# Spread rows of a four-layer graph attention kernel: through DRAM and ScalarE instead of TensorE transposes

## The chip, the cores and the metric

The kernel runs on one core of a Trainium2 chip. A core has five engines, each with its own in-order queue of instructions: TensorE (PE, matrix products and transposes; its weight loads are listed as PEld), VectorE (DVE), ScalarE (ACT), GpSimd (POOL) and SyncE (SP), which here issues every transfer. They work on SBUF (128 partitions) and on PSUM, where TensorE leaves its results; the DMA engines move data between SBUF and DRAM. The metric is the device time of one execution in microseconds, lower is better.

## What is computed

x is (32, 512, 256), float32: 32 graphs (batches) of 512 nodes with 256 features; adj is one 512x512 matrix of 0 and 1 for all of them. Four layers of graph attention follow each other, each on a normalised input and with a residual:

```python
h = jnp.maximum(_layernorm(x, axis=-1), 0.0)
x = x + layer(h, adj, ...)

# layer 0: four heads of 64 features, slope 0.2
e = s_src[:, :, None, :] + s_dst[:, None, :, :]
e = jnp.where(e > 0, e, 0.2 * e)
e = jnp.where(mask, e, -jnp.inf)
alpha = jax.nn.softmax(e, axis=2)
out = elu(einsum('bijh,bjhd->bihd', alpha, Wh))

# layer 1: a dense layer to 512, attention over all nodes (no mask) on 512 features,
# elu, residual, a dense layer to 256, attention with the mask, elu, residual, relu
# layer 2: one head of 256, slope 0.2, mask with the diagonal, elu
# layer 3: one head of 256, slope 0.01, mask, relu
```

Each attention weight is exp(leaky(s_i + t_j) + mask_ij - peak_i), divided by its sum over j. s and t are one number per node, two columns of a product with the layer's weights.

## The kernel before

**Tiles.** A batch stands in SBUF as 128 partitions x 4 tiles of nodes x 256 features (`xt`). Its numbers per node (s, t and what follows from them) are columns: 128 partitions x 4. To add s_i and t_j for a whole 128x512 tile of weights, one of the two must lie along the free dimension in all 128 partitions: a *spread row*, 128x512, each partition with the same 512 numbers.

**Two ways to a spread row.** `spread` (L632) makes it with TensorE: four transposes (L409) of a column, broadcast to 128x128, into a PSUM tile `row`. `lines` (L638) with `row_of` (L652) makes it through DRAM: one transpose (L643) turns the columns into a few partitions, ScalarE copies them to SBUF (`turned`), SP writes them to DRAM as `line` (L647), and SP reads the line back, broadcast to 128 partitions, into an SBUF tile `rb` of 256 KB (L655).

**Where they are used, per batch.**
- `peaks` (L658): spread of t, then for each of four node tiles one VectorE instruction (L665) that adds the mask and takes the maximum. Called for each of four heads, and once in each of three `gat`.
- `weights_T` (L694): `row_of` for cb (slope x s - top), spread for ca (s - top). For each of four tiles VectorE (L708) makes max(ca + (1 - slope) t, cb), GpSimd (L718 or L726) adds the mask, ScalarE (L719 or L733) takes the exponential into `pt`, which is the next product's weights. Called once a head and once a `gat`.
- `full_gat_T` (L838, no mask): the maximum of t over all nodes by a reduction (L859), one broadcast transpose and another reduction (L862); then `low_row` through DRAM and `t_row` by transposes (L886, L887) from the exponentials `c`; after the sums, `r_row` through DRAM and `q_row` by transposes (L908, L909).

The columns themselves come from `score_columns` (L678). Products are issued by `product` (L413); a product of 32-bit numbers is two matmul instructions in the profile, a transpose is one.

**The order.** Nothing is issued as the functions call it. `do` records each operation with its engine and an estimated duration, and `Plan.order` (L211) plays the recording: five batches are admitted at a time (`DEPTH`), each engine takes the ready operation with the lowest key, and tiles come from pools with a fixed number of slots (`SLOTS`: 7 of PSUM, 14 of the kind that holds `rb` and `y`). Keys are `max(0, b - 1) * PERIOD - urgency - add` with one urgency per operation of a batch (`URGENCY`, `FIRST` for the first graph recorded, and `EARLY` and `LAST` for the first and last three batches). The result is one fixed order for each engine. A matmul that is followed in this play by a gap of PE of at least 400 ns gets fillers, transposes of the identity into a PSUM tile that nothing reads (L1040):

```python
before.fill = int(FILL * gap / FILL_NS) if gap >= FILL_FROM else 0   # 0.6, 110, 400
```

A transfer is played with `max(n / 290, 300)` ns on SP, and lands 2500 ns later (900 for one of up to 8 KB).

Of the kernel before, what the change touches and what calls it, by code (L numbers as in the profile page):

```python
# [17 lines left out]
P = 128  # L18
# [18 lines left out]
PERIOD = 102900  # L37
# [7 lines left out]
    124187, 27458, 54024, 85815, 127927, 143082, 328815, 201328, 391462, 117691, 172181, 188793, 424644,  # L45
    248357, 290339, 151093, 548898, 347549, 249382, 346103, 190819, 493927, 189995, 235067, 375057, 312531,
    137476, 244237, 15588, 99471, 384419, 49912, 229134, 263406, -53868, 164326, 315017, 150418, 189541,
    87635, 113355, 113764, 92446, 180536, 315464, 22239, 104163, 37445, 153709, 69377, -33292, 57871, 68049,
    126632, 69380, 719561, 411345, -24739, 362683, 348747, 125710, 203386, -121226, 187184, 138735, 353972,
    479768, 379305, 100152, 225429, 177495, 202483, 437896, 179455, 177379, 459436, 207363, 251462, 276418,  # L50
    273051, 72134, 190340, 87240, 87462, 139994, 240070, 193165, 284099, 65171, 190882, -134531, 105489,
    204215, 436695, 354960, 84403, 365091, 388125, 158735, 132975, 125189, 140317, 28490, 135519, -133251,
    154984, 88833, 200704, 326910, 157401, -73420, 186088, 84030, 65473, 259435, 167820, 250548, 296226,
    155732, 148751, 184404, 102606, 47275, -89101, 109929, -22866, 120917, 132180, 72833, 179715, 293811,
    220306, 251604, 160377, -54812, 503963, 294348, 299648, 310480, 184310, 214427, 108134, 113382, 77944,
    -25259, 220915, 140253, 225101, 210070, 131593, -58641, 24901, 144922, 103834, -55042, -75773, 164955,
    51925, 37449, -37331, 194373, 165595, -53550, 134891, 73360, 200944, 169423, 370536, 148147, -8567,
    38227, 46537, -53506, 90629, 156363, 38013, 136307, 242309, 268100, 181379, 540681, 343781, 13085,
    106358, 381623, 252693, 34895, 86342, 41729, 145874, 57439, 180188, 371373, 144376, 113078, 212804,
    -56127, 175395, 39766, 20079, 122711, 16968, 81730, 36363, 33992, -9360, 244377, -16060, 173755, 812,  # L60
    195516, 96125, 24952, -99232, -256301, -273097, -325559, -217701, 62283, 41197, -317611, 121173,
    -573678, 24884, 161520, 281482, 42489, 132062, -71349, 206084, 127481, 161080, 218323, 174535, 382862,
    102363, 138949, -461371, 156706, 104313, 110685, 23741, 36809, 245583, 241597, 127455, 108694, 188549,
    189532, 121772, -38178, 162471, 73800, -52269, -68603, 102738, -10655, -40955, 2651, -65771, -94520,
    -132306, -380612, -101522, 98486, -36866, 305416, 62454, 65218, 94847, 204499, -47196, -74891, 216006,
    116703, -2381, -35719, -54275, -88533, -61935, 162867, -43915, 33052, -66202, 300499, -32636, 366366,
    327210, 59123, -165649, -89201, -347471, -174109, 44450, -340320, -322205, 336730, 425930, -331413,
    -60472, 15548, -236854, 64799, -286767, 264655, 136916, -210240, -130968, -69939, 4579, -163881,
    -114273, 229104, -3917, 51351, -164012, 71327, 184751, 34354, 88349, 218844, 73114, -114468, -63532,
    -85563, 244008, -87751, 209096, 276106, 219920, -137361, -89605, -131850, 241785, 82900, -208551,  # L70
    408441, 219935, -120937, -86266, -303126, 83675, 342059, 247005, 270933, 343321, 445672, 32970, 226125,
    -99438, 421870, 210292, 244826, 111374, 326504, 91555, -198928, -201687, -117310, 106781, -204532,
    67380, 99851, 66174, 191938, 283427, -85698, 6999, -8041, -95104, 177690, 102217, 25471, -7218, -47609,
    83544, -176267, 249182, -156218, -42446, -271332, 96408, -67700, 346080, -176537, -62170, -305860,
    -184573, -145498, -147352, 117568, -69973, 118138, -249506, 368017, 13506, -339817, -119489, 20691,
    -348133, -79577, -84578, 6007, 307149, -307611, -145956, -183471, -15732, 140957, -255635, -382374,
    11304, -58674, 49007, 69987, -197223, -465279, -170466, -47363, -177944, -100942, -227476, -459555,
    -35943, -374495, -161886, -188736, -213550, -478756, -113477, -237771, 114174, 25915, -203660, -235706,
    -62347, -49597, -119568, -276148, -278214, -571867, -240723, -472941, -276555, -150856, -178488,
    -125457, 51835, -119700, -113894, -198170, -267546, 913, 117494, 256204, 145580, 376286, 209102, 171461,  # L80
    165583, 1669, 258510, 19824, 278900, -103101, 178925, -9332, -105670, 172239, -297204, -161311, 107839,
    -80060, -168358, -503089, 286564, 116767, -326016, 36349, -42523, -373280, 52721, -549613, -185149,
    -350665, -263248, -524205, -114044, -425175, -394279, -290405, -98380, -283605, -656628, -503163,
    -332603, -466007, -238943, -479060, -312439, -461877, -761392, -824734, -834926, -757956, -1420966,
    -867896, -996520, -1174568, -1123798, -565242, -880525, -1056087, -1150294, -548818, -562165, -896349,
]
FIRST = [
    150625, 66367, -80914, 492852, 578582, 373790, 355233, 415411, 370342, 690632, 394774, 315517, 353203,
    129880, 197161, 432376, 789236, 500119, 645039, 728290, 726809, 782644, 812030, 1227229, 554726, 440195,
    427374, 520046, 670466, 709727, 194712, 543582, 496069, 321884, 91730, -45145, -92106, -199160, -149565,  # L90
    -369576, -525217, 119569, -25360, -315873, -515466, -503797, -111924, -325457, -83298, -69769, -254726,
    -424755, -154683, -114778, -101144, -419674, -490772, -341279, -218775, -354199, -315242, -499839,
    -403835, -279297, -179333, -63778, -215266, -305608, -132642, -176645, -343457, -55095, -344188, -79362,
    -182571, -64104, -353103, 2550, -407651, -228043, -371846, -353326, -107818, -171068, -352557, 71238,
    -155665, -77756, 69351, 83846, -64981, -152757, -173901, -107973, -117670, -664153, -331667,
# [3 lines left out]
    [350911, 4027, 95729, 276014, 659, -22230, 139089, 81698],  # L99
    [64803, 14957, 3729, -92060, -58664, 505679, 18595, -112320],  # L100
    [19486, -119307, -73079, 207604, 52200, 207194, -142315, -3205],
]
LAST = [
    [221588, 144111, 158140, 151755, 738851, -328217, 140264, 837366],
    [95908, 48069, 135713, 252237, -167477, -708999, 206689, 139833],
    [-4997, 24600, 39765, 70813, -84122, 447504, -165822, -554656],
# [226 lines left out]
def gat_stack(  # L333
# [298 lines left out]
    def spread(cols, holds=()):  # L632

        row = Later("ps", "row", [P, N])
        transposes(row.all, [cols(t).view(lambda a: a.to_broadcast([P, P])) for t in range(NT)], holds)
        return row

# [14 lines left out]
    def row_of(line, n):  # L652

        row = Later("b2", "rb", [P, N])
        transfer(row.all, [line[n : n + 1]], 4 * P * N, lambda o, a: nc.sync.dma_start(out=o, in_=a.to_broadcast([P, N])))  # L655
        return row

    def peaks(t_col, far, peak):  # L658

        row = spread(t_col)  # L660
        for it in range(NT):
            left = Later("b1", "left", [P, N], BF16)

            def run(o, junk, a, far):
                return nc.vector.tensor_tensor_reduce(  # L665
                    out=junk,
                    in0=a,
                    in1=far,
                    scale=1.0,
                    scalar=LOWEST,  # L670
                    op0=ALU.add,
                    op1=ALU.max,
                    accum_out=o,
                )

            do(DVE, 690, [peak(it), left.all], [row.all, far[:, it, :]], run)

    def score_columns(s, t, peak, lift, slope, shape):  # L678
# [3 lines left out]
        u, top, ca, cb, cc, ct = (Later("tiny", n, [P, *shape]) for n in ("u", "top", "ca", "cb", "cc", "ct"))  # L682
# [5 lines left out]
        do(DVE, 78, [ca.all], [s, top.all], lambda o, a, b: nc.vector.tensor_tensor(o, a, b, ALU.subtract))  # L688
        do(DVE, 78, [cb.all], [s, top.all], lambda o, a, b: stt(o, a, slope, b, ALU.mult, ALU.subtract))
        do(POOL, 200, [cc.all], [t], lambda o, a: nc.gpsimd.tensor_scalar(o, a, 1.0 - slope, None, ALU.mult))  # L690
        do(POOL, 200, [ct.all], [t], lambda o, a: nc.gpsimd.tensor_scalar(o, a, slope, None, ALU.mult))
        return ca, cb, cc, ct

    def weights_T(ca, line_b, cc, ct, farT, even):  # L694

# [395 lines left out]
```

## Time and profile before

Three runs took 3389.28, 3391.61 and 3391.96 us. One more execution was profiled.

| what | value |
|---|---|
| median of the runs | 3391.61 us |
| the profiled execution, its own time | 3391.39 us |
| its span, first to last instruction | 3389.6 us |
| mean granted TensorE clock | 0.999 |
| PE busy in the first 100 us | 81.22 us |
| PE busy in the last 40 us (3350 to 3390) | 32.13 us |
| PE busy from 500 to 3000 us | 2491.92 of 2500 us |
| `rb` rows read back, 256 KB each | 288 |
| `line` writes, 2 KB / 8 KB | 160 / 32 |
| row transposes of L409 | 2080 |
| line transposes of L643 | 192 |
| share of 16 DMA engines in the middle | 0.11, 34 GB/s |

How to read the lines below: a group line gives the source line, the engine, the operation, what is written from what, the shapes and the count, then busy microseconds, the mean duration of one in ns, and the idle time of the engine just before these instructions with what ended it. A timeline line gives start, duration, engine and group. A waits line gives the waiting instruction, what ended the wait, and the total, the number and the longest of such waits in microseconds. A matmul's duration holds the time in which the next ones already run behind it.

### The profile page before, as it was taken

How to read it: one execution, taken by the hardware profiler on the slowest of the kernel's cores; microseconds unless marked ns; L12 is line 12 of the kernel's file. 1: busy time of each engine (PE TensorE's matmuls, PEld its weight loads, DVE VectorE, ACT ScalarE, POOL GpSimd, SP SyncE). 2: the span in 40 equal slices, each digit the busy share in tenths (PEclk: the TensorE clock that was granted, in tenths of full speed). 3: DMA queues.
4: the chain of work that ended last, by engine and by line, in shares of the span. 5: the costliest groups of instructions: out<-in, count | busy, mean ns of one | idle time of the engine just before them, and what ended most of it. 6: DMA issues, size and time to landing. Idle time of an engine off the chain costs nothing. (4 is left out here: it accounts for less than half of the span.)

```text
span 3389.6 us, 52024 instructions
## 1 busy us (share of the span) xinstructions
PE 3348.1 (99%) x17313; PEld 2610.8 (77%) x17313; DVE 2732.0 (81%) x8008; ACT 2122.0 (63%) x4269; POOL 1483.5 (44%) x1801
## 2 busy tenths in 40 slices
PE   7999999999999999999999999999999999999998
PEld 7867777777777777877778777777877788777777
DVE  8777788888878888878888878888887888789576
ACT  4556666666666666665676565666665666666565
POOL 4433444344444445443445443444443454454244
PEclk9999999999999999999999999999999999999999
DMA  3000011101110101101011101011101011110011
GB/s 125 32 10 29 27 40 29 38 23 38 41 38 29 35 26 38 41 32 33 25 36 42 38 29 38 23 38 42 38 29 35 23 41 39 35 40 23 13 32 35
DMA packets 82828, 118.76 MB, mean 35 GB/s; under 512 B 7808, under 2 KB 44288, under 8 KB 82560
## 3 DMA queue, kind: packets, MB, share of 16 engines
q1 hardware_dynamic: 82560, 115.44, 10.9%
q8 instruction: 137, 2.24, 0.3%
q14 instruction: 131, 1.07, 0.1%
HBM read 98.04 MB, written 17.37 MB: 34 GB/s over the span
## 5 line engine op out<-in xcount | busy, mean ns | idle before, releaser
L726 POOL TENSOR_TENSOR y<-y,farT_some 128x512 f32<-128x512 f32 x512 | 591.4, 1180 | 375.7 <-DVE y L708 372.9
L419 PE MATMUL mm<-v,pt 128*128 128x257 f32 x3072 | 698.8, 381 | 1.4 <-ACT pt L719 0.5
L708 DVE SCALAR_TENSOR_TENSOR y<-row,cc,rb 128x512 f32<-128x512 f32 x896 | 619.5, 741 | 48.8 <-DMA rb<-line 40.7
L419 PEld LDWEIGHTS mm<-v,pt 128*128 128x128 f32 x3072 | 571.4, 190 | 89.5 <-ACT pt L719 4.2
L733 ACT ACTIVATE pt<-y,ct 128x512 f32<-128x512 f32 x640 | 455.9, 716 | 149.1 <-POOL y L726 141.7
L419 PEld LDWEIGHTS mmh<-vh,pt 128*128 128x128 f32 x4096 | 482.7, 192 | 10.2 <-ACT pt L733 3.7
L419 PE MATMUL mmh<-vh,pt 128*128 128x65 f32 x4096 | 484.7, 272 | 1.9 <-ACT pt L733 1.8
L419 PE MATMUL mm<-wfc,out1T 128*128 128x256 f32 (+1 forms) x2048 | 468.6, 380 | 0.0
L419 PE MATMUL mm<-ptf,hfc 128*128 128x512 f32 x1024 | 456.8, 594 | 0.0
L665 DVE CUSTOM_DVE_ANT_0 left<-row,far_nz 128x512 bf16<-128x512 f32 x640 | 416.3, 683 | 25.0 <-PE row L409 24.4
L718 POOL TENSOR_TENSOR y<-y,g 128x512 f32<-128x512 f32 x256 | 328.9, 1302 | 243.8 <-ACT g L714 214.3
L419 PEld LDWEIGHTS mm<-wfc,out1T 128*128 128x128 f32 x2048 | 380.6, 189 | 51.7 <-issue 0.5
L624 ACT ACTIVATE h<-xt,shift,rstd 128x256 f32<-128x256 f32 x512 | 275.6, 592 | 173.6 <-DVE shift L616 166.3
L419 PEld LDWEIGHTS mm<-ptf,hfc 128*128 128x128 f32 x1024 | 187.9, 190 | 199.9 <-issue 192.1
L726 POOL TENSOR_TENSOR y<-y,farT_self 128x512 f32<-128x512 f32 x128 | 146.2, 1165 | 409.9 <-DVE y L708 402.4
L419 PE MATMUL mm<-hT,w 128*128 128x512 f32 x512 | 229.3, 593 | 0.2 <-DVE hT L1037 0.2
L419 PE MATMUL mm<-out1T,wm 128*128 128x512 f32 x512 | 225.4, 592 | 0.2 <-ACT out3T L953 0.2
L1037 DVE BATCH_NORM_STATS2 stats<-xt 128x6 f32<-128x256 f32 x512 | 204.1, 410 | 6.5 <-DMA xt<-in_x_dram 5.1
L882 ACT ACTIVATE ra<-rb,c 128x512 f32<-128x512 f32 x256 | 177.6, 715 | 35.1 <-DMA rb<-line 34.9
L609 POOL TENSOR_SCALAR rstd<-mv 128x4 f32<-128x4 f32 x128 | 37.9, 296 | 369.1 <-DVE mv L1037 286.0
L854 ACT ACTIVATE hfc<-mm 128x256 f32<-128x256 f32 x128 | 48.4, 378 | 218.0 <-PE mm L419 210.2
L419 PEld LDWEIGHTS mm<-out1T,wm 128*128 128x128 f32 x512 | 96.7, 190 | 109.1 <-issue 99.8
(154 smaller groups left out, 5720.3 us busy)
## 6 DMA issues: line engine op xcount, KB each, us to landing
rb<-line SPq DMA_DIRECT2D x288, 256.0 KB
xt<-in_x_dram SPq DMA_DIRECT2D x32, 512.0 KB
out_dram<-xt SPq DMA_DIRECT2D x32, 512.0 KB
line<-turned SPq DMA_DIRECT2D x160, 2.0 KB
adj_sb<-in_adj_dram SPq DMA_DIRECT2D x1, 1024.0 KB
wfc<-in_L_gnn_W_fc_dram SPq DMA_DIRECT2D x2, 512.0 KB
a_row<-in_L_gnn_a_dram SPq DMA_DIRECT2D x3, 256.0 KB
wm<-in_L_gnn_mlp_w_dram SPq DMA_DIRECT2D x1, 512.0 KB
```

The costliest lines, as they stand in the source:

```text
L419: nc.tensor.matmul(o, lhsT=parts[k], rhs=parts[nk + k], start=(k == 0), stop=(k == nk - 1))
L609: do(POOL, 200, [rstd.all], [mv[:, :, 1]], lambda o, a: nc.gpsimd.tensor_scalar(o, a, EPS, None, ALU.add))
L624: lambda o, a, m, s: nc.scalar.activation(o, a, AF.Relu, bias=m, scale=s),
L665: return nc.vector.tensor_tensor_reduce(out=junk, in0=a, in1=far, scale=1.0, scalar=LOWEST, op0=ALU.add, op1=ALU.max, accum_out=o,)
L708: lambda o, a, c, b: nc.vector.scalar_tensor_tensor(o, a, c, b, ALU.add, ALU.max),
L718: do(POOL, 1255, [y.all], [y.all, g.all], lambda o, y, g: nc.gpsimd.tensor_tensor(o, y, g, ALU.add))
L726: lambda o, y, far: nc.gpsimd.tensor_tensor(o, y, far, ALU.add),
L733: lambda o, a, c: nc.scalar.activation(o, a, AF.Exp, bias=c),
L854: do(ACT, 300, [v], [mm[:, :HF]], lambda o, a: nc.scalar.activation(o, a, AF.Copy, bias=1.0))
L882: lambda o, a, k: nc.scalar.activation(o, a, AF.Copy, scale=k),
L1037: made = p.run(*(r.ap() if isinstance(r, Ref) else r for r in p.args))
```

## The change

1. `spread` is removed. In its place `psum_row_of` reads a row back from a DRAM line and lets ScalarE copy it from SBUF to PSUM, where the users find it as before.
2. `peaks` gets its row from outside. The four heads share one line of t; each `gat` writes one of its own.
3. `score_columns` writes ca and cb side by side into `cab`, so that one line transfer carries both; `weights_T` reads its two rows from it.
4. `full_gat_T` reads the raw t back as a row, takes the maximum over the row in one VectorE instruction, and makes `t_row` (in PSUM) and `low_row` by two exponentials on ScalarE. The row q comes through DRAM with r.
5. With `behind`, the rows of heads 2 and 3 wait for the peaks or weights of the head two before.
6. `PERIOD`, `URGENCY`, `FIRST`, `EARLY` and `LAST` have new numbers.

Per batch this makes 24 rows read back (9 before), 10 line writes (6 before), no row transposes (65 before), 10 line transposes (6 before), 15 row copies and 2 row exponentials on ScalarE. The changed program holds 976 fillers, the one before 385.

```diff
-PERIOD = 102900
+PERIOD = 97000
...
-    def spread(cols, holds=()):
-
-        row = Later("ps", "row", [P, N])
-        transposes(row.all, [cols(t).view(lambda a: a.to_broadcast([P, P])) for t in range(NT)], holds)
-        return row
...
-    def row_of(line, n):
+    def row_of(line, n, behind=()):
 
         row = Later("b2", "rb", [P, N])
-        transfer(row.all, [line[n : n + 1]], 4 * P * N, lambda o, a: nc.sync.dma_start(out=o, in_=a.to_broadcast([P, N])))
+        transfer(
+            row.all,
+            [line[n : n + 1], *behind],
+            4 * P * N,
+            lambda o, a, *_: nc.sync.dma_start(out=o, in_=a.to_broadcast([P, N])),
+        )
         return row
 
-    def peaks(t_col, far, peak):
-
-        row = spread(t_col)
+    def psum_row_of(line, n, holds=(), behind=()):
+
+        row = Later("ps", "row", [P, N])
+        do(ACT, 570, [row.all], [row_of(line, n, behind).all], nc.scalar.copy, holds)
+        return row
+
+    def peaks(row, far, peak):
+
...
-        u, top, ca, cb, cc, ct = (Later("tiny", n, [P, *shape]) for n in ("u", "top", "ca", "cb", "cc", "ct"))
+        u, top, cc, ct = (Later("tiny", n, [P, *shape]) for n in ("u", "top", "cc", "ct"))
+        cab = Later("tiny", "cab", [P, 2, *shape])
+        ca, cb = cab[:, 0], cab[:, 1]
...
-    def weights_T(ca, line_b, cc, ct, farT, even):
+        return cab, cc, ct
+
+    def weights_T(line, at, cc, ct, farT, even, behind=()):
...
-        rb = row_of(*line_b)
-        row_a = spread(ca, [pt])
+        rb = row_of(line, at[1], behind)
+        row_a = psum_row_of(line, at[0], [pt], behind)
...
-        peaks(lambda t: v[:, t, D + 2 : D + 3], far, lambda it: peak[:, it : it + 1])
+        peaks(psum_row_of(lines(v[:, :, D + 2], 1), 0), far, lambda it: peak[:, it : it + 1])
...
-        line_b = lines(cb.all, 1)
-        ca, *cs = (lambda t, c=c: c[:, t : t + 1] for c in (ca, *cs))
-        pt = weights_T(ca, (line_b, 0), *cs, farT, not own)
+        line = lines(cab.all.view(lambda a: a.rearrange("p x t -> p (x t)")), 2)
+        cs = (lambda t, c=c: c[:, t : t + 1] for c in cs)
+        pt = weights_T(line, (0, 1), *cs, farT, not own)
...
+        line = lines(st[:, 1].view(lambda a: a.rearrange("p h t -> p (h t)")), H)
         for hd in range(H):
-            peaks(lambda t: st[:, 1, hd, t : t + 1], far, lambda it: peak[:, hd, it : it + 1])
-        ca, cb, *cs = score_columns(st[:, 0], st[:, 1], peak.all, None, slope, [H, NT])
-        line_b = lines(cb.all.view(lambda a: a.rearrange("p h t -> p (h t)")), H)
+            behind = [peak[:, hd - 2, :]] if hd > 1 else []
+            peaks(psum_row_of(line, hd, (), behind), far, lambda it: peak[:, hd, it : it + 1])
+        cab, *cs = score_columns(st[:, 0], st[:, 1], peak.all, None, slope, [H, NT])
+        line = lines(cab.all.view(lambda a: a.rearrange("p x h t -> p (x h t)")), 2 * H)
+        begun = []
         for hd in range(H):
-            ch, *cs_h = (lambda t, c=c: c[:, hd, t : t + 1] for c in (ca, *cs))
-            pt = weights_T(ch, (line_b, hd), *cs_h, farT, False)
+            cs_h = (lambda t, c=c: c[:, hd, t : t + 1] for c in cs)
+            behind = [begun[hd - 2].all] if hd > 1 else []
+            pt = weights_T(line, (hd, H + hd), *cs_h, farT, False, behind)
+            begun.append(pt)
...
-        tmax = Later("tiny", "tmax", [P, 2])
-        do(DVE, 78, [tmax[:, 0:1]], [t], lambda o, a: nc.vector.tensor_reduce(o, a, AX.X, ALU.max))
-        row = Later("ps", "row", [P, P])
-        transposes(row.all, [tmax[:, 0:1].view(lambda a: a.to_broadcast([P, P]))])
-        do(DVE, dve(P), [tmax[:, 1:2]], [row.all], lambda o, a: nc.vector.tensor_reduce(o, a, AX.X, ALU.max))
-        tmax = tmax[:, 1:2]
+        raw = row_of(lines(t, 1), 0)
+        tmax = Later("tiny", "tmax", [P, 1])
+        low_max = Later("tiny", "low_max", [P, 2])
+        do(DVE, 600, [tmax.all], [raw.all], lambda o, a: nc.vector.tensor_reduce(o, a, AX.X, ALU.max))
+        for k, slope in enumerate((1.0, 0.2)):
+            do(
+                DVE,
+                78,
+                [low_max[:, k : k + 1]],
+                [tmax.all],
+                lambda o, a, x=-slope: nc.vector.tensor_scalar(o, a, x, None, ALU.mult),
+            )
+        t_row, low_row = Later("ps", "t_row", [P, N]), Later("b2", "low_row", [P, N])
+        for k, (o, slope) in enumerate(((t_row, 1.0), (low_row, 0.2))):
+            do(
+                ACT,
+                615,
+                [o.all],
+                [raw.all, low_max[:, k : k + 1]],
+                lambda o, a, m, x=slope: nc.scalar.activation(o, a, AF.Exp, bias=m, scale=x),
+            )
+        tmax = tmax.all
...
-        low_row = row_of(lines(c[:, 3, :], 1), 0)
-        t_row = spread(lambda t: c[:, 2, t : t + 1])
...
-        r_row = row_of(lines(rq[:, 0, :], 1), 0)
-        q_row = spread(lambda t: rq[:, 1, t : t + 1], [pt])
+        line = lines(rq.all.view(lambda a: a.rearrange("p x t -> p (x t)")), 2)
+        r_row = row_of(line, 0)
+        q_row = psum_row_of(line, 1, [pt])
```

## The prediction

> **What bounds the kernel now.** The page's first part comes first: the share of each engine. Then one batch cut out of the middle, where the chain of waits repeats every 102.5 us (its piece of 48 matmuls starts at 2168.75, 2271.20, 2373.70, 2476.29).
>
> ```profile
> PE 3348.1 (99%) x17313; PEld 2610.8 (77%) x17313; DVE 2732.0 (81%) x8008; ACT 2122.0 (63%) x4269; POOL 1483.5 (44%) x1801
> ```
> ```profile
> 2171.20:2273.70 102.50, 102.50 (x529) 80.00 (x528) 84.49 (x249) 65.91 (x133) 46.30 (x56) 1.00 0.11 34
> ```
> The second line gives, after the length of the stretch, the busy time of PE, PEld, DVE, ACT and POOL, the granted clock, the DMA share and GB/s. PE is busy in all of 102.50 us; DVE has 18.0 us free, ACT 36.6, POOL 56.2. A busy PE need not be a full one, so I read the pace of its matmuls from the timeline: four row transposes start at 1504.39 and the next work at 1504.82, eight start at 1539.45 and the next at 1540.33. That is 0.109 us each, though each lasts 0.273.
>
> ```profile
> 1504.39 0.60 PE L409 MATMUL row<-ident,ca 128*128 128x128 f32 x4
> 1504.82 1.90 PE L419 MATMUL mm<-v,pt 128*128 128x257 f32 x8
> ...
> 1539.45 1.04 PE L409 MATMUL row<-ident,ca 128*128 128x128 f32 x8
> 1540.33 7.03 PE L419 MATMUL mm<-ptf,hfc 128*128 128x512 f32 x16
> ```
> By the same reading 24 of mmh take 2.63 us, 24 of 128x257 5.22 and 16 of 128x512 6.87. Per batch that is 128 x 0.110 + 224 x 0.218 (forms of 256 to 264) + 64 x 0.429 + 111 transposes x 0.109 = 102.4 us: in the middle PE is packed, and a matmul taken away is time. 32 batches take 3280.0 of the 3389.6 us; 109.6 lie at the ends: first matmul at 8.96 and last end at 3384.3 (14 us), 64 mask transposes (7), 385 fillers at 0.109 (42.0), and 46.6 of waits and slow first matmuls.
>
> **The change, part by part.** (1) Matmuls. The spread rows are 65 transposes a batch:
>
> ```profile
> L409 PE MATMUL row<-ident,ca 128*128 128x128 f32 x896 | 130.1, 273 | 5.2 <-DVE y L708 3.2 <-DVE ca L688 1.1 <-DVE peak_h L665 0.8
> ...
> L409 PE MATMUL row<-ident,st 128*128 128x128 f32 x512 | 71.0, 273 | 0.2 <-ACT farT_some L1037 0.2
> ...
> L409 PE MATMUL row<-ident,v 128*128 128x128 f32 x384 | 58.3, 273 | 0.5 <-DVE v L1037 0.3 <-ACT v L1037 0.2
> ...
> L1040 PE MATMUL filled<-ident 128*128 128x128 f32 x385 | 50.5, 279 | 0.0
> ```
> With rq 128, c 128 and tmax 32 they are 2080, and 2080 x 0.109 = 226.7 us. The changed program's list has none of them. Its line transposes are 320 where there were 192: 128 x 0.109 = 14.0 us. Net -212.7, or 102.5 to 95.85 us a batch.
>
> (2) Fillers. The changed program issues 976 where there were 385: about 355 near the start, 300 near the end, and 12 in every batch between. Running them costs 591 x 0.109 = +64.4. They stand at gaps of the new order, and what else such gaps hold is bounded from both sides: nothing, or what a filler has beside it now, 46.6 / 385 = 0.121, so 0 to +72. Line 327 covers six tenths of a gap, which leaves 0.4/0.6 x 0.109 = 0.073 per filler: +43, between the ends. Below nothing would be fillers in idle time that was there already; it can give back at most the 46.6.
>
> (3) ScalarE. Per batch 15 copies of a row to PSUM, two exponentials of a row and four more line copies. No copy from SBUF to PSUM is in the trace; the nearest rows are 575 ns (hT from PSUM) and 716 (pt with a pointer). 15 x 0.575 to 0.716 is 8.6 to 10.7; the exponentials 2 x 0.63 to 0.72, 1.3 to 1.4; the line copies 4 x 0.25. Together 10.9 to 13.1; I take 12, and ACT goes from 65.9 to 78 of some 98 us. On the path: nothing. If the cover were gone, all 12 x 32 = 384 us would show.
>
> ```profile
> L733 ACT ACTIVATE pt<-y,ct 128x512 f32<-128x512 f32 x640 | 455.9, 716 | 149.1 <-POOL y L726 141.7 <-POOL v L758 0.5
> ...
> L1037 ACT COPY hT<-tr 128x512 f32<-128x512 f32 x128 | 73.6, 575 | 9.9 <-PE tr L409 8.4
> ```
> (4) VectorE. The maximum over a whole row (0.60 to 0.74 by ef L933 and y L708) and two small products (0.17 each) come, two reductions (0.156, 0.290) go: +0.5 to +0.6, so 85.1 of 98, 87%. Covered by PE's 95.85 while the order holds; POOL is unchanged.
>
> (5) Transfers. Rows of 256 KB go from 9 to 24 a batch (288 to 768 in all), lines from 6 to 10; all stand on SP's one queue. SP's own time is 24 x 0.32 + 10 x 0.26 + 0.8 = 11 us a batch. The DMA share goes from 0.11 to about 0.25: no bound. What it adds is lateness. Two trips, one on an idle queue (timeline) and one behind other rows (chain of waits):
>
> ```profile
> 2021.51 0.26 SPq L647 DMA_DIRECT2D line<-turned  x1
> ...
> 2023.06 0.33 SPq L655 DMA_DIRECT2D rb<-line  x1
> ```
> ```profile
> 2105.55 2.60 DMA line<-turned
> 2108.17 3.39 DMA rb<-line
> ```
> The line lands 1.29 us after its issue ends on the idle queue, 2.60 after it began on the busy one; the row takes 3.39. With transpose, line copy and row copy a spread takes 6 to 7.5 us where four transposes took 0.6. Four stages of a batch (the peaks of the heads and of three gats) get this trip new. The weights waited for the same line already and get one copy more; line 858's maximum gets a trip, and the low row's trip goes in exchange. So one batch alone is some 4 x 6 + 5 = 29 us longer. Five batches in flight cover it in the middle; what shows at the ends is in (2).
>
> A late row stops what stands behind it: on ACT the exponentials and line copies of other batches, for which POOL, PE and SP then wait; on SP all later rows, the x loads and stores. Today's price:
>
> ```profile
> DVE y L708 <- DMA rb<-line: 40.7, 50, 2.7
> ACT ra L882 <- DMA rb<-line: 34.9, 32, 4.6
> ```
> (in all, times, longest). 75.6 us over 288 rows, 0.26 a row; 480 more rows make 126 us of such waits on ACT and DVE. Upper end: PE passes all of it on, +126. Lower end: none. A gain has no way to arise from a later row. In the window above PE lost nothing to them, which is nearer the lower end: +14.
>
> **Sum:** 3389.6 - 212.7 + 64.4 + 43 + 14 = 3298. The profiled execution took 3391.4, 1.8 more than its span, and the median of the runs shown is 3391.6: 3300 us, 2.7% faster.
>
> **The rivals.**
> A, packed: the fillers run and nothing else is lost, 3389.6 - 212.7 + 64.4 + 2 = 3243. For it: PE's idle time in the middle was zero. Against: the new order has gaps in every batch, and ACT's and DVE's free time shrinks to 20 and 13 us.
>
> B, late rows through the middle: all 126 us of (5) reach PE but the gaps of (2) stay: 3241 + 43 + 126 + 2 = 3412 at most, half of it 3349. For it: DVE at 87%, so a stop is not made up quickly. Against: five batches of work on every queue.
>
> C, slower, one mechanism: ACT's queue stops at the row copies. Its work is 78 a batch; each of 15 copies that waits w adds 15 w. It decides from 102.5 = 78 + 15 w, w = 1.64 us. If each copy pays the line's delay under load (2.60 - 1.29 = 1.31) and the mean of a row wait where there is one (75.6 / 82 = 0.92), w = 2.23, the batch is 111.4 us, and 32 x 111.4 + 109.6 = 3675. For it: lines were at 1.29 calm and 2.60 and 3.04 behind rows, and rows come in groups of four to six now. Against: 206 of 288 rows had landed unwaited, and the DMA share stays at a quarter. The Trainium skill's page HBM Reference, section Latency, gives 0.2 us for an access on average and 2 us at high load; the line rows agree that load adds more than a microsecond, and by that rule alone every line of this rival would be late. No run here shows the load of the changed kernel.
>
> D, no change: PE's saved time would have to turn up as 6.65 us of idle time in every batch; the transposes are gone from the program, so only waits could do that. 3392.
>
> **How the numbers follow.** Forecast (3300, own range 3265 to 3330) 0.55; A 0.25; B 0.11; C 0.07; D 0.02. The range goes down to 3225, below A, for fillers that partly stand in idle time already there (18 of the 46.6), and up to 3385, past B's half; outside remain C, D and small parts of A and B. A measurement of this kernel can tell about 0.2% from no change (6.8 us). Faster: forecast, A and B, 0.91; same D, 0.02; slower C, 0.07.
>
> **What would show it.** (1): no group of row matmuls; PE's count down by 2080 - 128 - 591 = 1361; a batch in the middle near 98 us (95.85 of work, 1.3 of fillers, the rest gaps). (2): more idle PE than the 18.8 us of the first 100 and the 7.9 of the last 40. (3): a row copy at 0.57 to 0.72 and ACT near 78%. (4): DVE near 87%. (5): 768 rows; waits of ACT for rows under 1 us each. Wrong: a middle batch above 100 us with ACT's row copy as the largest wait for DMA (B, C), or one below 97.2 with the fillers running in it (A).

## The result and the profile after

| | before | changed |
|---|---|---|
| median of the runs | 3391.78 us (4 runs, 3389.28 to 3396.86) | 3310.58 us (4 runs, 3307.18 to 3314.17) |
| span of the profiled execution | 3389.6 us | 3312.5 us |

The ratio is 0.9759, with a 95% interval of 0.9742 to 0.9776: 2.4% faster. The page of the changed kernel begins so (busy time, share of the span, count):

```profile
PE 3228.9 (97%) x15952; PEld 2475.6 (75%) x15952; DVE 2689.0 (81%) x8040; ACT 2410.0 (73%) x4941; POOL 1474.0 (44%) x1801
...
q1 hardware_dynamic: 155008, 242.29, 24.1%
```

PE has lost 1361 instructions, and its share has fallen from 99% to 97%: it is no longer packed. Transfers are at 24.1% of the DMA engines. For the middle, take the 21 batches between the fifth and the 26th store of an output. Of the changed kernel, and then of the kernel before (PE, PEld, DVE, ACT, POOL, granted clock, DMA share, GB/s after the length):

```profile
772.58:2855.15 2082.57, 2060.97 (x10041) 1574.79 (x10041) 1744.50 (x5229) 1571.17 (x3235) 959.80 (x1176) 1.00 0.25 76
```
```profile
801.34:2962.80 2161.46, 2153.48 (x11061) 1677.40 (x11059) 1779.56 (x5203) 1382.19 (x2787) 971.38 (x1175) 1.00 0.11 34
```

A middle batch takes 2082.57 / 21 = 99.17 us where it took 102.93. ScalarE is at 74.8 us a batch (75%), VectorE at 83.1 (84%).

Busy time hides where PE waits with a matmul still in its pipe, so I counted the matmuls of each form in each stretch and multiplied by its pace (0.109 us a transpose or filler, 0.110 a matmul of 65 columns, 0.004 + 0.00083 us per column for the wider ones). "Rest" is the length less work and fillers: idle time, pipeline ends and slow clock.

| us | length | PE work | fillers | rest |
|---|---|---|---|---|
| before, up to the fifth store | 801.3 | 746.6 | 22.2 | 32.5 |
| before, 21 batches | 2161.5 | 2149.2 | 0.5 | 11.7 |
| before, from the 26th store on | 426.8 | 390.0 | 19.2 | 17.6 |
| changed, up to the fifth store | 772.6 | 671.5 | 44.1 | 57.0 |
| changed, 21 batches | 2082.6 | 2012.4 | 27.0 | 43.1 |
| changed, from the 26th store on | 457.3 | 389.0 | 35.2 | 33.1 |

In all the work fell by 212.9 us, fillers rose by 64.4 and the rest by 71.4; that is the 77.1 by which the span fell. So two thirds of what TensorE was spared went into gaps. At the ends they took all of it: the 21 middle batches are 78.9 us shorter, while the two ends together are 1.8 us longer (28.7 less up to the fifth store, 30.5 more from the 26th on), although 76 us of PE work left them.

One such gap, in the timeline of the changed kernel (start, duration, engine, line, operation; in brackets the idle time before it):

```profile
1481.43 0.41 DVE L1066 COPY v<-mm 128x258 f32<-128x258 f32 x1
...
1481.89 0.72 PE L1069 MATMUL filled<-ident 128*128 128x128 f32 x5
...
1483.09 0.40 DVE L1066 COPY v<-mm 128x258 f32<-128x258 f32 x1
...
1483.63 0.27 PE L640 MATMUL tr<-ident,v 128*4 128x128 f32 x1 [1.03 <-ACT ra L912]
...
1483.74 1.03 PE L1069 MATMUL filled<-ident 128*128 128x128 f32 x8
...
1484.88 0.70 PE L422 MATMUL mm<-v,pt 128*128 128x257 f32 x2
...
1486.02 4.17 PE L422 MATMUL mm<-v,pt 128*128 128x257 f32 x18 [0.43 <-ACT pt L742]
```

The one line transpose of t needs all four copies of `v`; two are VectorE's, and the second starts at 1483.09, behind layernorm statistics of another batch. PE's next place in the order is that transpose, so it runs five fillers and waits 1.03 us, then runs eight more fillers until an exponential is ready: some 3 us of PE, 1.4 of them filled. The profile puts the end of this wait down to a ScalarE instruction that ended 0.11 us after the copy. But the transpose starts 0.145 us after the copy's end, as it does in nearly all waits at this place that the profile puts down to the copy. Over the whole execution those are PE's largest wait (us in all, times, longest):

```profile
PE tr L640 <- DVE v L1066: 15.7, 26, 1.1
```

In the 21 middle batches PE is idle for 2082.57 - 2060.97 = 21.6 us. Of these 14.6 stand before the line transposes of `v`, three a batch (the numbers behind the last bar), and 174 of the 248 fillers there run just before or behind them:

```profile
L640 PE MATMUL tr<-ident,v 128*4 128x128 f32 x63 | 17.4, 276 | 14.6 <-DVE v L1066 11.5 <-ACT pt L742 2.0 <-ACT ra L912 1.0
```

### The profile page after: what moved, and what is told of

Its sections match the earlier page's. It is cut to its first block, busy times and chain, and to the rows that moved or that the text cites. A ratio compares the mean times of both kernels' runs of the same rounds, so it can differ in the third digit from the quotient of the medians.

```text
span 3312.5 us, 51505 instructions
## 1 busy us (share of the span) xinstructions
PE 3228.9 (97%) x15952; PEld 2475.6 (75%) x15952; DVE 2689.0 (81%) x8040; ACT 2410.0 (73%) x4941; POOL 1474.0 (44%) x1801
## 3 DMA queue, kind: packets, MB, share of 16 engines
q1 hardware_dynamic: 155008, 242.29, 24.1%
## 5 line engine op out<-in xcount | busy, mean ns | idle before, releaser
L735 POOL TENSOR_TENSOR y<-y,farT_some 128x512 f32<-128x512 f32 x512 | 580.3, 1163 | 351.6 <-DVE y L717 335.5
L422 PEld LDWEIGHTS mm<-v,pt 128*128 128x128 f32 x3072 | 574.5, 190 | 117.8 <-ACT pt L728 14.5
L727 POOL TENSOR_TENSOR y<-y,g 128x512 f32<-128x512 f32 x256 | 321.0, 1282 | 384.4 <-ACT g L723 243.8
L422 PE MATMUL mm<-wfc,out1T 128*128 128x256 f32 (+1 forms) x2048 | 461.3, 380 | 2.4 <-ACT hfc L868 2.1
L1066 ACT COPY row<-rb 128x512 f32<-128x512 f32 x480 | 279.1, 584 | 97.6 <-DMA rb<-line 86.6
L1012 POOL TENSOR_TENSOR rz<-rz,res 128x256 f32<-128x256 f32 x128 | 97.8, 764 | 304.1 <-ACT rz L991 269.7
L672 DVE CUSTOM_DVE_ANT_0 left<-row,far_pos 128x512 bf16<-128x512 f32 x256 | 168.6, 675 | 7.1 <-ACT row L1066 7.1
L1066 ACT COPY turned<-tr 8x128 f32<-8x128 f32 (+3 forms) x320 | 76.2, 246 | 129.3 <-PE tr L640 129.0
```

The lines of the kernel that those rows point to most:

```text
L422: nc.tensor.matmul(o, lhsT=parts[k], rhs=parts[nk + k], start=(k == 0), stop=(k == nk - 1))
L672: return nc.vector.tensor_tensor_reduce(out=junk, in0=a, in1=far, scale=1.0, scalar=LOWEST, op0=ALU.add, op1=ALU.max, accum_out=o,)
L727: do(POOL, 1255, [y.all], [y.all, g.all], lambda o, y, g: nc.gpsimd.tensor_tensor(o, y, g, ALU.add))
L735: lambda o, y, far: nc.gpsimd.tensor_tensor(o, y, far, ALU.add),
L1012: do(POOL, 685, [r], [r, res[:, it, :]], lambda o, a, b: nc.gpsimd.tensor_tensor(o, a, b, ALU.add))
L1066: made = p.run(*(r.ap() if isinstance(r, Ref) else r for r in p.args))
```

## The experiments

Each kernel is compared with the kernel before on the same chip. A difference to the changed kernel is the difference of the two ratios times 3392 us; since each ratio is known to about 0.2%, so is the difference to some 8 to 10 us. The diffs show the main lines of each edit.

**1. PE's work put back.** The changed kernel, with transposes of the identity added:

```diff
-        do(PE, 110, [tr.all], [cols], lambda o, a: nc.tensor.transpose(o, a, ident))
+        def turn(o, a):
+            return [nc.tensor.transpose(o, a, ident)] + [nc.tensor.transpose(filled, ident, ident) for _ in range(6)]
+
+        do(PE, 110, [tr.all], [cols], turn)
```

> The changed kernel with six more transposes of the identity behind each line transpose (60 a batch, nearly the 61 that the change took away); order, rows, copies and transfers as they are. PE theory (PE's own stream sets the pace in the middle, and the removed transposes were worth their 0.109 us each): 1920 x 0.109 = 209 us more, less what falls into the 1.5 us of idle time and tails that a middle batch has (up to 48 us): 3470 to 3520 us, a middle batch near 104.5. Lateness theory (late rows or a full ScalarE set the pace, and PE has room): at most 40 us more, below 3350, a middle batch below 100.

3461.7 us, ratio 1.020 (1.0184 to 1.0215): 150 us more than the changed kernel for 209 us of work, 0.72 of each. A middle batch is 104.34 us. The lateness theory as put here, with room on PE, falls; the PE theory is 8 us outside its range. The rest in the 21 middle batches fell from 43.1 to 14.3 us, so the gaps took in part of the work.

**2. The peaks' rows without the wait for the line.** Seven of 24 rows a batch are read from x; the maxima are then over other numbers.

```diff
-            lambda o, a, *_: nc.sync.dma_start(out=o, in_=a.to_broadcast([P, N])),
+            lambda o, a, *_: nc.sync.dma_start(out=o, in_=(a if still is None else still).to_broadcast([P, N])),
...
+    still = x[0, 0:2].rearrange("(o a) f -> o (a f)", o=1)
```

> The changed kernel with the seven rows a batch that the peaks read taken from the first two rows of x in DRAM instead of the line: they no longer wait for a transpose, a copy and a line write (the lines are still written; the peaks are maxima over other numbers). Order and counts are the same. PE theory: the middle keeps its 98.7 us within 0.5, and only the ends gain, 5 trips of some 3 us at each: 3270 to 3310 us. Lateness theory (the new trips ate the 50 us beyond the fillers and gaps of the forecast): 3220 to 3260, a middle batch near 97.2.

3308.4 us, 0.9757 (0.9733 to 0.9782), a middle batch 99.29: no difference. The expectation said more than the edit does: the line's write still stands ahead of the row on SP's queue and waits there for the transpose and the copy (SP's waits for `turned` come to 1975.2 us, 1896.0 in the changed kernel). Run 6 takes that away too.

**3. No fillers.**

```diff
-FILL, FILL_NS, FILL_FROM = 0.6, 110, 400
+FILL, FILL_NS, FILL_FROM = 0.0, 110, 400
```

> The changed kernel with no fillers (FILL 0.0, 976 matmuls fewer), nothing else. The forecast counted their running as +64 us: if they delay what follows, 3311 - 106 x 0.6 to 1.0 = 3205 to 3250 us. If they stand in gaps that are there anyway: unchanged, 3305 to 3320. If they keep PE's clock up: the granted clock falls below the 0.994 of the changed kernel, and the time rises, 3330 to 3420.

3346.1 us, 0.9856 (0.9840 to 0.9873): 33 us more, and the granted clock is 0.967 (0.994 with fillers). The third case. On balance fillers cost nothing here; they stand in gaps that exist and keep the clock up. In the trace 222 us ran at half clock, 42 in that of the changed kernel.

**4. The matmuls taken away alone.** The kernel before, its order and all else kept, with one transpose per spread row:

```diff
-        row = Later("ps", "row", [P, N])
-        transposes(row.all, [cols(t).view(lambda a: a.to_broadcast([P, P])) for t in range(NT)], holds)
+        row = Later("ps", "row", [P, 1, P])
+        def run(o, *parts):
+            return [nc.tensor.transpose(o[:, 0, :], parts[0], ident)]
+        cols4 = [cols(t).view(lambda a: a.to_broadcast([P, P])) for t in range(NT)]
+        do(PE, 109.2 * NT, [row.all], cols4, run, holds)
```

> The kernel before with one transpose per spread row instead of four (512 x 3 + 48 are left out of 2080: 1536 fewer); VectorE reads the one block of 128 columns four times over, so that the rows hold the first node tile only. Order, fillers, all else as before. PE theory: 1536 x 0.109 = 167 us fewer if the order of before lets PE run ahead, 3225 us; with the other engines' waits coming up, 3225 to 3290. Rival (ScalarE, VectorE or GpSimd are close behind, and what the change gave back was never to be had): 3320 to 3390.

3341.8 us, 0.9839 (0.9821 to 0.9858): 55 us fewer for 167 us of work (1536 transposes; the 48 more in the expectation were not left out), 0.33 of each. (The users' instructions keep their durations: 740 ns for `y`, 741 before.) The rival's range. PE's largest wait has grown:

```profile
PE tr L409 <- ACT h L624: 46.2, 34, 8.9
```

(us in all, times, longest; 17.4 in 14 before). So in this fixed order the matmuls of a packed PE are not worth their time: PE runs ahead to the next step that another engine feeds, and stops.

**5. Row copies made twice.**

```diff
-        do(ACT, 570, [row.all], [row_of(line, n, behind).all], nc.scalar.copy, holds)
+        def twice(o, a):
+            return [nc.scalar.copy(o, a), nc.scalar.copy(o, a)]
+
+        do(ACT, 570, [row.all], [row_of(line, n, behind).all], twice, holds)
```

> The changed kernel with each copy of a row to PSUM made twice (480 more ScalarE copies of 0.58 us, 8.7 us a batch); order and all else as they are. The forecast called the copies covered by PE: ScalarE then goes from 76% to about 84% of a batch of 99 us. Covered: within 15 us of the changed kernel, 3300 to 3325. ScalarE theory (its in-order queue is what leaves PE the 1.5 us of idle time and tails in a middle batch): each added copy delays what stands behind it, a third or more of 8.7 x 32 = 279 us shows: above 3400. Between them: 3325 to 3400, and the price of a copy is read from it.

3464.8 us, 1.0207 (1.0171 to 1.0242): 152 us more for 480 copies of 0.58 (279 us), 0.54 of each. "Covered" falls, though ScalarE was busy only 75% of a middle batch. With it, PE waits for exponentials where it hardly did:

```profile
PE mmh L422 <- ACT pt L745: 33.7, 40, 2.0
```

It was 7.9 us in 9 waits in the changed kernel.

**6. The peaks' rows without the line at all.** As run 2, and the line isn't written:

```diff
         def run(o, a):
+            if unwritten:
+                return []
             return nc.sync.dma_start(out=o.rearrange("n (t p) -> (n t) p", p=P), in_=a)
```

> As the run without the wait for the line, and the line of t that the peaks would read isn't written either (128 transfers fewer, and SP has nothing of them to wait for): the seven rows of the peaks are taken from x and depend on no transpose, line copy or SP wait. Lateness theory in its last form (SP's queue stands before the line writes and holds the rows back): below 3280 us, a middle batch under 98. Order theory (the fixed order of PE, ScalarE and VectorE has the gaps; transfers are early enough): 3295 to 3320, a middle batch of 98.5 to 99.2.

3312.9 us, 0.9757 (0.9737 to 0.9777), a middle batch 99.16: no difference again. The copies' waits for rows fell from 86.6 to 58.4 us (38.8 for rows of lines, 19.6 for rows of x), and nothing came of it: what lateness of the peaks' rows was taken away cost nothing that these runs can tell. PE still waits for `v` ahead of the transpose, which is made though no line comes of it: 19.7 us in 32 waits, the largest of its waits.

**7 and 8. More fillers.** FILL 1.0, and FILL 0.8 from gaps of 200 ns on.

> The changed kernel with fillers for the whole of each gap (FILL 1.0: 1647 instead of 976), nothing else. Clock theory (the changed kernel's trace has 42 us at half clock, costing 21 us of work, and the run with more transposes had only 5.5): the granted clock rises to 0.998 or more, 3290 to 3305 us. Filler cost theory (fillers run past their gaps): 671 x 0.109 = 73 us more at most, 3315 to 3385.

> The changed kernel with fillers for eight tenths of each gap of 200 ns or more (1352 of them in 153 places instead of 976 in 119). Clock theory: the granted clock at 0.997 or more, 3290 to 3305 us. Filler cost theory: 376 x 0.109 = 41 us more at most, 3315 to 3350.

3320.0 us, 0.9776 (0.9761 to 0.9790), clock 1.000; and 3315.3 us, 0.9759 (0.9745 to 0.9774), clock 0.998. The clock came up as expected in both, 3.5 us at half clock in run 7, and neither is faster; run 7 is 6 us above the changed kernel, inside what these runs can tell. A middle batch stays at 99.20 in both. So the slow clock was not what held the time up: with it gone, the span has 242.6 us beside PE's work in run 7, and 239.6 in the changed kernel.

**9. Row copies cut to a quarter.** One block of 128 columns is copied, VectorE reads it four times over:

```diff
-        row = Later("ps", "row", [P, N])
-        do(ACT, 570, [row.all], [row_of(line, n, behind).all], nc.scalar.copy, holds)
+        row = Later("ps", "row", [P, 1, P])
+        def part(o, a):
+            return nc.scalar.copy(o[:, 0, :], a[:, 0:P])
+        do(ACT, 570, [row.all], [row_of(line, n, behind).all], part, holds)
```

> The changed kernel with each of the 480 row copies cut to its first 128 columns (some 0.25 us by the line copies, instead of 0.58); VectorE reads that block four times over, so the rows hold the first node tile only. It leaves out 0.33 x 15 = 5 us of ScalarE a batch; order and all else as they are. ScalarE theory (the run with the copies made twice paid 0.54 of every added microsecond): 5 x 0.54 x 32 = 85 us less, 3215 to 3240, a middle batch near 96.5, which with 95.85 of work and 1.31 of fillers is about the floor, so 3240 to 3260 if the fillers bind first. Order theory (the gaps are fixed by PE's and VectorE's places in the order; more ScalarE work hurts, less doesn't help): 3290 to 3315.

3294.8 us, 0.9708 (0.9692 to 0.9724): 17 us fewer, within the order theory's range and far from the ScalarE theory's. ScalarE's busy time for these copies fell from 279.1 to 125.4 us, so 0.11 of each microsecond came out, where run 5 paid 0.54. A middle batch is 98.57.

**10 and 11. Without a searched order.** In both kernels:

```diff
-            urgency = URGENCY if b else FIRST
+            urgency = [0] * len(pieces)
...
-            add = more[b][n * len(more[b]) // len(pieces)] if b in more else 0
+            add = 0
```

> The kernel before with every urgency and every addition for first and last batches at zero, so that keys are batch and place in the recording alone (its own PERIOD kept). Measures what its searched order is worth: somewhere from 3450 to 4000 us, PE with gaps in every batch.

> The changed kernel with every urgency and addition at zero, as the run beside it. If the way of making rows is better by itself (fewer matmuls count without a searched order too): faster than the unsearched kernel before by 1 to 6%. If the change rests on its order (the longer trips are only hidden by it): slower than the unsearched kernel before by 1% or more.

3890.0 us (ratio 1.1467, 1.1444 to 1.1490) and 3895.3 us (1.1482, 1.1448 to 1.1517), two runs each. Neither case: with keys of batch and place alone the two ways of making rows are equal within the intervals. The searched orders are worth about 500 and 585 us; the whole change is 81.

**12. VectorE relieved.** The maxima of the peaks over 128 columns, with the identity for the mask:

```diff
-                    out=junk,
-                    in0=a,
-                    in1=far,
+                    out=junk[:, 0:P],
+                    in0=a[:, 0:P],
+                    in1=ident,
```

> The changed kernel with the maxima of the peaks over 128 columns instead of 512 and with the identity in place of the mask (28 VectorE instructions of 0.68 us a batch become about 0.25): it leaves out three quarters of each maximum and the mask in it, some 12 us of VectorE a batch, 384 in all; VectorE goes from 84% to 72%. Order and all else as they are. VectorE theory (its queue at 84% is what leaves PE the gaps that less ScalarE work did not close): a middle batch near 97.2, where work and fillers bind, 3240 to 3270 us. Order theory (PE's gaps stand in the fixed order between steps that depend on each other, and lighter engines close little of them): 3285 to 3310, a middle batch of 98 to 99.

3309.1 us, 0.9737 (0.9717 to 0.9757), a middle batch 99.03. The groups of VectorE's maxima, here and in the changed kernel (the last has a second group of 256):

```profile
L672 DVE CUSTOM_DVE_ANT_0 left<-row,ident 128x128 bf16<-128x128 f32 x896 | 228.2, 280 | 59.6 <-ACT row L1066 58.7
```
```profile
L672 DVE CUSTOM_DVE_ANT_0 left<-row,far_nz 128x512 bf16<-128x512 f32 x640 | 416.4, 681 | 23.9 <-ACT row L1066 23.2
```

VectorE's busy time fell by 305 us (2689.0 to 2384.1, 72%), the time by some 7, no more than these runs can tell; VectorE's idle time before the maxima grew from 31 us, with both groups, to 59.6. The VectorE theory falls.

**What they say together.** In the changed kernel's order an added microsecond costs 0.72 on PE and 0.54 on ScalarE; one taken away gives 0.11 on ScalarE and 0.02 on VectorE, the last within the noise; the trip of the peaks' lines and the clock give nothing. Neither ScalarE nor VectorE is the bound by its load. PE is near it: a middle batch has 2012.4 / 21 = 95.83 us of PE work and 3.3 beside it, of which no relief tried gave back more than 0.6. What is left is the order: each engine's fixed queue, in which a step waits for one particular step of another. The trace shows this for the wait for `v`; for the other gaps it is argued by elimination, and neither GpSimd's work nor the lateness of the other 17 rows of a batch was taken away. It was not shown by a better order for the changed kernel; whether there is one stays open.

Runs 10 and 11 say one thing more. Without a searched order the 1952 fewer transposes gain nothing, and the change came with new numbers for the order. How much of the 81 us belongs to the rows and how much to the new order is not shown.

The fastest of these kernels that computes the whole reference is the changed one; run 8 equals it.

## Why the prediction was right, point by point

The forecast was 3300 us, its own range 3265 to 3330; 3310.6 came. In spans the sum was 3298 and 3312.5 came, 14.5 us more.

1. **Matmuls, -212.7.** Counted in the trace, -212.9. No group of row transposes is left, and the count fell by exactly 1361. The reading of the pace from starts instead of durations (0.109 against 0.273 us) holds. But "a matmul taken away is time" does not follow from a packed PE: run 4 got 0.33 of it in an order made for the old durations, and between runs 10 and 11, where PE is not packed (run 10 has a span of 3888.4 us for 3285.8 us of PE work), the same matmuls gave nothing.
2. **Fillers +64.4, and +43 beside them.** Fillers 64.4, as their number in the program said. The rest rose by 71.4, where the sum had 57: 43 here and 14 for late rows in (5). That is the term that was mis-sized. It came out at the upper bound of 72 that the rows gave for the gaps alone. The bounds were 0 to 72 and 0 to 126, and little spoke for 43 and 14 between them, so that the sum came so near is in part luck. Their name was wrong as well. Run 3 shows that fillers are no cost: 64.4 + 71.4 = 135.8 us are gaps of the new order, part of them filled. The sign named for them came: PE is idle for 25.6 us of the first 100 (18.8 before) and 8.7 of the last 40 (7.9).
3. **ScalarE, "on the path: nothing".** The size was near. The copy is at 584 ns, by the low row (575) of the two that bounded it:

```profile
L1066 ACT COPY row<-rb 128x512 f32<-128x512 f32 x480 | 279.1, 584 | 97.6 <-DMA rb<-line 86.6 <-DVE peak_h L672 4.3 <-DVE stats L1066 1.9
```

   ScalarE went to 74.8 us a batch instead of 78. That they cost nothing holds only nearly: run 9 finds 17 us for a little more than half of them, and run 5 shows that there is no cover for more.
4. **VectorE, +0.5 a batch.** It fell, from 84.7 to 83.1 us a batch in the 21 middle batches. Three groups with two inputs in SBUF got shorter (lines 971, 972 and 984: 343.1 us in all, now 265.1), as the last section describes; others got longer. It decides nothing (run 12).
5. **Transfers, +14 for late rows.** Counts as forecast. Runs 2 and 6 find 0 for the peaks' rows, seven of the 24; the others' lateness was not taken away, so the 14 for all of them stays untested. ScalarE waited for a row at 96 of 480 copies, 0.90 us each. Lines are hardly later than before: SP's waits for their landing average 1.15 us (1.09 before, 205.0 / 188):

```profile
SPq L656 <- DMA line<-turned: 327.7, 286, 4.1
```

   So the 2.60 taken from the busy queue was not typical.

**The rivals.** A, packed at 3243: no, the gaps are there, 3.3 us of them in a middle batch. B, late rows through the middle: neither its 3349 nor its 3412 came, the copies' waits for rows are 86.6 us in all, and runs 2 and 6 gain nothing by freeing seven rows of 24. C, ScalarE's queue stopped at the copies: a copy waits 86.6 / 480 = 0.18 us on average, far from the 1.64 from which it decides. The rule cited with it is the Trainium skill, HBM Reference, section Latency: 2 us an access at high load. The lines' 1.15 us at a DMA share of 0.25 do not show that state. D, no change: no. Yet ScalarE, the engine of C, has little to spare: run 5 adds 8.7 us of ScalarE work to a batch and is slower than the kernel before.

## What to carry to other kernels

When every engine runs a fixed queue, the load of an engine may tell little of what a change on it is worth: measure the price by putting work back and by taking it away, since the two can differ, by a factor of five on ScalarE here. Count the work of the packed engine before and after by its paces; what the count saves and the time does not is in gaps, and a table by stretch shows where. Fillers that a program puts where its plan has gaps tell of those gaps, and are to be priced as gaps, not as work. And where a new order comes with a change, the total does not tell how much of the gain is the order's.

## What the runs showed of the hardware that was not expected

**VectorE's durations depend on what runs beside it.** The same instruction on the same sizes, before and after:

```profile
L984 DVE SCALAR_TENSOR_TENSOR ez<-ez,rz 128x256 f32<-128x256 f32 x128 | 92.2, 722 | 36.8 <-ACT ez L982 23.1 <-POOL xt L994 12.3 <-POOL rz L983 1.2
```
```profile
L1013 DVE SCALAR_TENSOR_TENSOR ez<-ez,rz 128x256 f32<-128x256 f32 x128 | 53.0, 422 | 2.6 <-POOL rz L1012 2.5
```

722 ns became 422, while line 985's, also with two inputs in SBUF, went from 428 to 532 (L1014); `y`, with one input in PSUM, stayed at 741. In the trace before, 42 of the 128 at line 984 had no GpSimd instruction beside them and took 399 to 426 ns; the other 86 took up to 1379, 966 in the median. In the trace after, 33 at line 1013 had one beside them and none took more than 475, so it matters how the two meet. The Trainium skill's GPSIMD Engine Reference, section Specifications, says that GpSimd shares its SBUF interfaces with VectorE and names contention with VectorE instructions that have two SBUF inputs. The rows agree with it, though no run here took GpSimd away.

**The half clock costs less than its time.** 222 us at half clock instead of 42 (run 3, which also has no fillers) cost 33 us, and 3.5 us instead of 42 (run 7) gained nothing. A likely reason, not shown by itself, is that part of the slow time lies where PE would otherwise wait.

**An exponential into PSUM was a little faster here.** Two exponentials read the same row, one into PSUM (`t_row`), one into SBUF (`low_row`): 679 and 709 ns. They also differ in scale and bias, and no run changed the target alone.
